# One planned, pinned order for every engine in a graph-attention plus gated-recurrence kernel

## The chip, the cores and the metric

The kernel runs on one core of a Trainium2 chip. A core has a matrix engine (TensorE, called PE in the profile, with its weight loads on a row called PEld), a vector engine (VectorE, DVE), a scalar engine (ScalarE, ACT), a general engine (GpSimd, POOL), and a sync engine (SyncE, SP) that here only issues transfers. The metric is the device time of one execution in microseconds (us). A span is one profiled execution, from its first to its last instruction.

## The reference, cut to what matters

There are 32 batch elements (B), each a table of 512 nodes by 128 features. One adjacency matrix of 512 by 512 zeros and ones serves all of them.

```python
# layer 0, for every batch element: graph attention
h = relu(layernorm(x))
hw = h @ W                                   # 512 x 128
logits = leaky_relu(hw @ a_src [rows] + hw @ a_dst [columns], 0.2)
alpha = softmax(logits where adj > 0)        # 512 x 512
x = x + leaky_relu(alpha @ hw + b, 0.3)
# layer 1, for every batch element: five gated recurrent steps
h = relu(layernorm(x))
for step in range(5):
    m = adj @ h
    z = sigmoid(m @ w3s.T + h @ u3.T)        # w3s: the two halves of w3 added, the same for w4, w5
    r = sigmoid(m @ w4s.T + h @ u3.T)
    hv = tanh(m @ w5s.T + (r * h) @ u5.T)
    h = (1 - z) * h + z * hv
out = x + h
```

The batch elements don't depend on each other, while the five steps of one element do. There are 160 such steps in all.

## The kernel before

**One step.** The state of an element is kept twice: transposed (`hT`, features on the partitions) and with nodes on the partitions, there split into a rounded part and the rest (`hi` and `lo`). `aggregate` multiplies `lo` and `hi` by the adjacency, eight matmuls into one PSUM bank (L573), and ACT copies the bank out as `mT` (L581). `gate_r` runs two products (L588, L589), a tanh (L591) and one vector operation that makes `rh` (L593). `candidate` adds the third product to the same bank (L599), takes its tanh (L603), and runs the two products of the candidate (L605, L606). `update` has one tanh (L614) and three vector operations that end in the new `hT` (L617 to L619). Then the state must be turned back to nodes on partitions. `turn` does it with four PE transposes (L635). `send` and `receive` do it with a vector transpose of 32 by 32 blocks (L643), one store to DRAM (L648) and four loads with rearranged addresses (L651), all on the SP queue. `halves` then makes `hi` on ACT (L419) and `lo` on DVE (L422), which the next `aggregate` reads.

**Layer 0** of an element is the generator `layer0`: a layer norm (L389 to L407, with one `pow` on POOL at L395), a transposition, a product (L474), scores `pt` (four vector operations, L511), the weighted average `av` (32 PE instructions, L528), its normalisation, a second layer norm, a second transposition and `halves`. The first four elements use PE transposes (`direct`); the others go through DRAM on the POOL queue (L431, L438), as does the row of exponentials `es` (L499, L504).

**What sets the order.** The driver at the end (L691 to L743) walks a software pipeline: in each turn one item is aggregated, the item before it goes through `gate_r`, the one before that through `candidate`, `update` and `send`, and after each third of a turn `advance` moves a layer 0 on by one piece. `WIDTH` = 6 elements run in the recurrence at once, `AHEAD` = 3 are in layer 0, and from `SENT` = 5 running elements on, the state is turned through DRAM. At the start three layer-0 generators are stepped in turn, `SKEW` = 3 pieces apart. This program order goes to the framework's scheduler, which makes each engine's instruction list from it with its own priorities and its own estimates of durations; only a few instructions are pinned to program order (`keep_in_program_order`: preparation of the adjacency, the input tests). Once made, the list of each engine is fixed, and an instruction that waits holds up those behind it in the list.

Of the kernel before, what the change touches and what calls it, by code (L numbers as in the profile page):

```python
# [21 lines left out]
SCORES = 25.0  # L22
WIDTH = 6
SENT = 5
SLOTS = 10
AHEAD = 3
DIRECT = 4
FIRST = 3
SKEW = 3
# [149 lines left out]
def gat_then_gated_gnn_kernel(  # L179
# [32 lines left out]
    xin = fast.enter_context(tc.tile_pool(name="xin", bufs=4))  # L212
    w2 = fast.enter_context(tc.tile_pool(name="w2", bufs=2))
    w3 = fast.enter_context(tc.tile_pool(name="w3", bufs=3))
    w4 = fast.enter_context(tc.tile_pool(name="w4", bufs=4))
    dram = fast.enter_context(tc.tile_pool(name="dram", bufs=4, space=bass.MemoryType.DRAM))
    psum = fast.enter_context(tc.tile_pool(name="psum", bufs=8, space=bass.MemoryType.PSUM))

    def bank(name):
        return psum.tile([P, N], F32, tag="bank", name=name)  # L220
# [11 lines left out]

    loaded = {}

    def load_x(b):
        if b < B:
            t = xin.tile([P, K, D], F32, tag="x", name=f"x_{b}")
            nc.sync.dma_start(out=t, in_=x_r[b])
            loaded[b] = t
# [21 lines left out]

    hws = [state.tile([P, K, D + 3], F32, name=f"hw_{s}") for s in range(AHEAD)]

# [9 lines left out]
    nc.scalar.dma_start(out=gw, in_=g_w)  # L273
    load_x(0)
    for i, v in enumerate((g_asrc, g_adst)):
        nc.scalar.dma_start(out=cols[:, i : i + 1], in_=v.rearrange("(d o) -> d o", o=1))
    nc.sync.dma_start(out=a_sb, in_=adj.rearrange("(p k) m -> p k m", k=K))
    load_x(1)
    nc.sync.dma_start(out=bias0, in_=g_b.partition_broadcast(P))
    load_x(2)  # L280
    for name, v in (("w3", w3_w), ("w4", w4_w), ("w5", w5_w)):
        nc.sync.dma_start(out=wide[name], in_=v)
    nc.sync.dma_start(out=u3, in_=u3_w)
    nc.sync.dma_start(out=u5, in_=u5_w)
    for i, v in enumerate((w3_b, w4_b, u3_b, w5_b, u5_b), 2):
        nc.sync.dma_start(out=cols[:, i : i + 1], in_=v.rearrange("(d o) -> d o", o=1))
    load_x(3)

    def prepare_layer0():

        wt_ps = bank("wt_ps")
        nc.tensor.transpose(wt_ps[:, :D], gw, ident)
        gwT = prep.tile([P, D], F32, name="gwT")
        nc.scalar.copy(gwT, wt_ps[:, :D])
        nc.gpsimd.tensor_copy(wrow[:, :D], gw)
        nc.gpsimd.tensor_copy(wsrc[:, :D], gw)
        wa_ps = bank("wa_ps")
        nc.tensor.matmul(wa_ps[:, 0:2], lhsT=gwT, rhs=cols[:, 0:2], start=True, stop=True)
        nc.scalar.copy(wa, wa_ps[:, 0:2])
        nc.scalar.copy(wrow[:, D : D + 1], wa[:, 1:2])  # L300
        nc.scalar.mul(wrow[:, D + 1 : D + 2], wa[:, 0:1], 0.8)
        nc.scalar.mul(wrow[:, D + 2 : D + 3], wa[:, 1:2], -0.8)
        nc.scalar.copy(wsrc[:, D : D + 1], wa[:, 0:1])
        nc.vector.tensor_scalar(wdst, ones, wa[:, 1:2], None, ALU.mult)

    def prepare_adjacency(c):

        at_ps = bank(f"at_ps{c}")
        for k in range(K):
            tc.keep_in_program_order(  # L310
                nc.tensor.transpose(
                    at_ps[:, ts(k, P)],
                    a_sb[:, k, :].rearrange("p (q c) -> p c q", c=K)[:, c, :],
                    ident,
                )
            )
        tc.keep_in_program_order(nc.vector.tensor_copy(adjT[:, c, :], at_ps))

    def prepare_layer1():


        sums = {}
        for name in ("w4", "w3", "w5"):
            sums[name] = prep.tile([P, D], F32, name=name + "s")
            nc.gpsimd.tensor_tensor(sums[name], wide[name][:, :D], wide[name][:, D:], ALU.add)
        nc.gpsimd.tensor_tensor(sums["w3"], sums["w3"], sums["w4"], ALU.subtract)
        t_ps = bank("w_ps")
        for i, name in enumerate(("w3", "w4", "w5")):
            nc.tensor.transpose(t_ps[:, ts(i, P)], sums[name], ident)
        nc.tensor.transpose(t_ps[:, ts(3, P)], u3, ident)  # L330
        for i, dst in enumerate((w3dT, w4sT, w5sT, u3T)):
            nc.scalar.copy(dst, t_ps[:, ts(i, P)])
        t_ps = bank("u5_ps")
        nc.tensor.transpose(t_ps[:, :D], u5, ident)

        tc.keep_in_program_order(
            nc.vector.tensor_scalar(u5hT, t_ps[:, :D], 0.5, None, ALU.mult)
        )
        tc.keep_in_program_order(
            nc.vector.tensor_scalar(zb, cols[:, 2:3], cols[:, 4:5], 0.5, ALU.add, ALU.mult)  # L340
        )
        tc.keep_in_program_order(
            nc.vector.tensor_scalar(rb, cols[:, 3:4], cols[:, 4:5], 0.5, ALU.add, ALU.mult)
        )
        tc.keep_in_program_order(
            nc.vector.tensor_tensor(vb, cols[:, 5:6], cols[:, 6:7], ALU.add)
        )

    def test_inputs():


        counts = prep.tile([P, 2 * K], F32, name="counts")
        for k in range(K):
            odd = w2.tile([P, N], F32, tag="d", name=f"odd_{k}")
            tc.keep_in_program_order(
                nc.vector.scalar_tensor_tensor(
                    odd, a_sb[:, k, :], 0.0, a_sb[:, k, :], ALU.not_equal, ALU.not_equal,
                    accum_out=counts[:, k : k + 1],
                )
            )  # L360
        deg = prep.tile([P, K], F32, name="deg")
        for k in range(K):
            tc.keep_in_program_order(
                nc.vector.tensor_reduce(
                    deg[:, k : k + 1], a_sb[:, k, :], mybir.AxisListType.X, ALU.max
                )
            )
        nc.vector.tensor_scalar(counts[:, K:], deg, 0.0, None, ALU.is_le)
        viol = prep.tile([P, 2], F32, name="viol")
        nc.vector.tensor_reduce(viol[:, 0:1], counts, mybir.AxisListType.X, ALU.add)  # L370
        wa2 = prep.tile([P, 2], F32, name="wa2")
        tc.keep_in_program_order(nc.vector.tensor_tensor(wa2, wa, wa, ALU.mult))
        nc.vector.tensor_reduce(viol[:, 1:2], wa2, mybir.AxisListType.X, ALU.add)
        return viol

    def conclude(viol):
        viol_ps = bank("viol_ps")
        nc.tensor.matmul(viol_ps[:, 0:2], lhsT=ones, rhs=viol, start=True, stop=True)
        over = prep.tile([P, 1], F32, name="over")
        nc.vector.tensor_scalar(over, viol_ps[:, 1:2], SCORES, None, ALU.is_gt)  # L380
        nc.vector.tensor_tensor(over, over, viol_ps[:, 0:1], ALU.add)
        nc.vector.tensor_scalar(flag, over, 0.0, None, ALU.is_gt)


    def relu_layernorm(dst, src, which, alone):
        st = w3.tile([P, K, 6], F32, tag="st", name=f"st_{which}")
        mv = w3.tile([P, K, 2], F32, tag="mv", name=f"mv_{which}")
        for k in range(K):
            nc.vector.bn_stats(st[:, k, :], src[:, k, :])  # L389
        for k in range(K):  # L390
            nc.vector.bn_aggr(mv[:, k, :], st[:, k, :])
        ve = w3.tile([P, K], F32, tag="ve", name=f"ve_{which}")
        nc.vector.tensor_scalar(ve, mv[:, :, 1], EPS, None, ALU.add)  # L393
        rs = w3.tile([P, K], F32, tag="rs", name=f"rs_{which}")
        nc.gpsimd.tensor_tensor(rs, ve, mhalf, ALU.pow)  # L395
        if alone:

            mean = mv[:, :, 0:1].to_broadcast([P, K, D])
            nc.vector.tensor_tensor(dst, src, mean, ALU.subtract)
            scale = rs.rearrange("p (k o) -> p k o", o=1).to_broadcast([P, K, D])  # L400
            nc.vector.scalar_tensor_tensor(dst, dst, 0.0, scale, ALU.max, ALU.mult)
            return

        nb = w3.tile([P, K], F32, tag="nb", name=f"nb_{which}")
        nc.vector.scalar_tensor_tensor(nb, mv[:, :, 0], -1.0, rs, ALU.mult, ALU.mult)
        for k in range(K):
            nc.scalar.activation(  # L407
                dst[:, k, :], src[:, k, :], AF.Relu, bias=nb[:, k : k + 1], scale=rs[:, k : k + 1]
            )

    def transposed(dst, src, which):
        t = bank(f"t_{which}")
        for k in range(K):
            nc.tensor.transpose(t[:, ts(k, P)], src[:, k, :], ident)
        nc.scalar.copy(dst, t)

    def halves(b, src, order="p k d -> p k d", **sizes):
        hi = his[b % SLOTS].rearrange(order, **sizes)
        nc.scalar.copy(hi, src)  # L419
        hi = his[b % SLOTS].bitcast(F32).rearrange(order, **sizes)  # L420
# [368 lines left out]
```

## Time and profile before

The median time is 1239.35 us (three runs, 1235.62 to 1241.69). The profiled span is 1236.1 us.

| engine | busy us | share of span | instructions |
|---|---|---|---|
| PE | 1168.6 | 95% | 4286 |
| PEld | 712.5 | 58% | 4286 |
| DVE | 936.7 | 76% | 2121 |
| ACT | 636.2 | 51% | 1260 |
| POOL | 346.5 | 28% | 496 |

Busy time by stage (us; the windows are cut from the start of the span):

| window | PE | DVE | ACT | POOL | granted PE clock |
|---|---|---|---|---|---|
| 0 to 100 | 73.23 | 61.39 | 45.35 | 24.36 | 0.96 |
| 100 to 250 | 134.80 | 101.25 | 68.74 | 42.73 | 0.96 |
| 250 to 1050 | 785.52 | 650.39 | 433.19 | 274.99 | 0.99 |
| 1050 to 1237 | 175.07 | 123.62 | 88.92 | 4.46 | 0.98 |

Busy time on PE counts overlapped matmuls generously: each of the 1280 instructions of L573 is shown as 399 or 474 ns long, while eight of them in a row take 1.84 us in the chain of waits.

### The profile page before, as it was taken

What the parts mean: (1) busy time and instruction counts of PE and PEld (TensorE: products, weight loads), DVE (VectorE), ACT (ScalarE), POOL (GpSimd) and SP (SyncE); (2) the same over time, 40 slices, a digit from 0 to 9 for tenths busy, and PEclk for the clock granted to TensorE, in tenths of its full rate; (3) what the DMA queues carried; (4) which work ended last, traced back from release to release, by engine and by line L of the source; (5) the groups of instructions that cost most, each with busy time, mean ns of one, the idle gap of its engine ahead of it and who ended that gap; (6) DMA issues with size and microseconds to landing.
All of it is one profiled execution on the core that took longest, in us unless ns stands there. A gap on an engine that the chain in (4) does not pass through costs nothing.

```text
span 1236.1 us, 15052 instructions
## 1 busy us (share of the span) xinstructions
PE 1168.6 (95%) x4286; PEld 712.5 (58%) x4286; DVE 936.7 (76%) x2121; ACT 636.2 (51%) x1260; POOL 346.5 (28%) x496
## 2 busy tenths in 40 slices
PE   6788887999999999999999999998999999999996
PEld 5555545655665655566566565655666666555553
DVE  5664667778788887888778887878888888766665
ACT  3454354455555555556544455555556545545552
POOL 2133132333334334233232333332332432100000
PEclk9899999999999999999999999999999999999998
DMA  3011123344444444353444443343443443322223
GB/s 95 20 44 34 26 61 111 111 129 119 135 129 129 128 120 131 103 146 106 126 122 128 140 127 116 113 136 112 128 130 118 128 120 113 109 94 85 86 88 119
DMA packets 134776, 133.40 MB, mean 108 GB/s; under 512 B 22432, under 2 KB 98592, under 8 KB 134560
## 3 DMA queue, kind: packets, MB, share of 16 engines
q1 hardware_dynamic: 116784, 95.54, 24.3%
q0 software_dynamic: 17472, 36.79, 12.0%
q8 instruction: 35, 0.57, 0.2%
q14 instruction: 53, 0.43, 0.1%
q10 hardware_dynamic: 432, 0.07, 0.0%
HBM read 70.65 MB, written 61.66 MB: 107 GB/s over the span
## 4 chain that ended last, share of the span: by engine, by line
PE 62%; DVE 17%; DMA 9%; POOL 4%; ACT 4%; issue 3%; SPq 1%; DVEq 0%; POOLq 0%; ACTq 0%
PE m L573 17%; PE g L588 8%; PE g L589 7%; PE v L606 7%; PE v L605 7%; PE g L599 7%; PE av L528 7%; DMA way<-blocks 3%; DMA rows<-way 3%; DVE lo L422 2%; DVE d L617 2%; DVE d L618 2%; DVE pt L511 2%; POOL rs_b L395 2%; DVE hT L619 1%
## 5 line engine op out<-in xcount | busy, mean ns | idle before, releaser
L573 PE MATMUL m<-adjT,lo 128*128 128x512 f32 x640 | 303.1, 474 | 25.8 <-DVE lo L422 25.8
L573 PE MATMUL m<-adjT,hi 128*128 128x512 f32 x640 | 255.3, 399 | 0.0
L591 ACT ACTIVATE rs<-g,rb 128x512 f32<-128x512 f32 x160 | 110.3, 689 | 150.9 <-PE g L589 148.5
L573 PEld LDWEIGHTS m<-adjT,lo 128*128 128x128 f32 x640 | 122.5, 191 | 89.0 <-DVE lo L422 32.0
L581 ACT COPY mT<-m 128x512 f32<-128x512 f32 x160 | 93.4, 584 | 148.5 <-PE m L573 148.1
L599 PE MATMUL g<-mT,w3dT 128*128 128x512 f32 x320 | 164.0, 594 | 1.7 <-ACT rs L591 1.6
L606 PE MATMUL v<-rh,u5hT 128*128 128x512 f32 x320 | 165.0, 597 | 0.0
L605 PE MATMUL v<-mT,w5sT 128*128 128x512 f32 x320 | 164.2, 595 | 0.0
L588 PE MATMUL g<-hT,u3T 128*128 128x512 f32 x320 | 164.1, 594 | 0.0
L589 PE MATMUL g<-mT,w4sT 128*128 128x512 f32 x320 | 163.4, 592 | 0.0
L593 DVE SCALAR_TENSOR_TENSOR rh<-rs,hT 128x512 f32<-128x512 f32 x160 | 108.0, 675 | 68.2 <-ACT rs L591 68.0
L614 ACT ACTIVATE hv<-v,vb 128x512 f32<-128x512 f32 x160 | 109.9, 687 | 93.4 <-PE v L606 92.3
L617 DVE TENSOR_TENSOR d<-hv,hT 128x512 f32<-128x512 f32 x160 | 109.3, 683 | 57.8 <-ACT hv L614 57.6
L528 PEld LDWEIGHTS av<-hw,pt 128*128 128x128 f32 x1024 | 129.0, 196 | 40.9 <-DVE pt L511 19.9
L573 PEld LDWEIGHTS m<-adjT,hi 128*128 128x128 f32 x640 | 122.8, 192 | 46.6 <-issue 23.1
L528 PE MATMUL av<-hw,pt 128*128 128x129 f32 x1024 | 132.7, 281 | 13.1 <-DVE pt L511 13.0
L395 POOL TENSOR_TENSOR rs_b<-ve_b,mhalf 128x4 f32<-128x4 f32 x32 | 36.4, 1137 | 344.5 <-DVE ve_b L393 222.6
L603 ACT ACTIVATE zs<-g,zb 128x512 f32<-128x512 f32 x160 | 110.1, 688 | 27.7 <-PE g L599 27.1
L419 ACT CAST hi<-rows 128x512 fp32r<-128x512 f32 x117 | 72.5, 619 | 87.1 <-DMA rows<-way 86.8
L619 DVE SCALAR_TENSOR_TENSOR hT<-d,hT 128x512 f32<-128x512 f32 x160 | 109.8, 686 | 9.0 <-DVE d L618 0.9
L618 DVE SCALAR_TENSOR_TENSOR d<-zs,d 128x512 f32<-128x512 f32 x160 | 109.7, 686 | 2.8
L643 DVE STREAM_TRANSPOSE blocks<-hT 128x512 f32<-128x512 f32 x147 | 103.9, 706 | 9.3 <-DMA way<-blocks 6.2
(115 smaller groups left out, 1391.2 us busy)
## 6 DMA issues: line engine op xcount, KB each, us to landing
way<-blocks SPq DMA_DIRECT2D x147, 256.0 KB, 2.1
rows<-way SPq DMA_DIRECT2D x588, 64.0 KB, 2.0
x<-in_x_dram SPq DMA_DIRECT2D x32, 256.0 KB, 2.7
out_dram<-res SPq DMA_DIRECT2D x32, 256.0 KB, 2.1
turn_a<-blocks_a POOLq DMA_DIRECT2D x112, 64.0 KB, 2.5
h0T<-turn_a POOLq DMA_DIRECT2D x28, 256.0 KB, 3.8
es<-line POOLq DMA_DIRECT2D x28, 256.0 KB, 3.9
turn_b<-blocks_b POOLq DMA_DIRECT2D x112, 64.0 KB, 2.4
```

The source lines that it names most:

```text
L528: nc.tensor.matmul(avs[:, i, :], lhsT=probs[c][:, ts(k, P)], rhs=hw[:, c, : D + 1], start=(c == 0), stop=(c == K - 1),)
L573: nc.tensor.matmul(m_ps, lhsT=part[b % SLOTS][:, k, :], rhs=adjT[:, k, :], start=(k == 0 and part is los), stop=(k == K - 1 and part is his),)
L588: nc.tensor.matmul(g_ps, lhsT=u3T, rhs=hT, start=True, stop=False)
L589: nc.tensor.matmul(g_ps, lhsT=w4sT, rhs=mT, start=False, stop=True)
L591: nc.scalar.activation(r, g_ps, AF.Tanh, bias=rb, scale=0.5)
L599: nc.tensor.matmul(g_ps, lhsT=w3dT, rhs=mT, start=False, stop=True, skip_group_check=True)
L603: nc.scalar.activation(z, g_ps, AF.Tanh, bias=zb, scale=0.5)
L605: nc.tensor.matmul(v_ps, lhsT=w5sT, rhs=mT, start=True, stop=False)
L606: nc.tensor.matmul(v_ps, lhsT=u5hT, rhs=rh, start=False, stop=True)
L617: nc.vector.tensor_tensor(d, hv, hT, ALU.subtract)
L618: nc.vector.scalar_tensor_tensor(d, z, 1.0, d, ALU.add, ALU.mult)
L619: nc.vector.scalar_tensor_tensor(hT, d, 0.5, hT, ALU.mult, ALU.add)
```

## The change

The driver, the generator and the lists of running elements go. Every piece of work becomes a `Task` with an engine, a length worked out from columns (`COST`: fixed nanoseconds, nanoseconds per column, time until the result is seen), a key (its urgency), the tasks it needs, and the buffers it takes or gives back. `plan` then plays the whole kernel through: it keeps a clock for each engine and a stock for each kind of buffer, always takes the engine that can begin first, and there, of the tasks that could begin at that moment, the one with the smallest key. The instructions are issued in that order, and all of them are pinned to it (`pin`), so that the framework's scheduler no longer chooses.

The computation stays the same. Besides the ordering, these details move: `aggregate` is two tasks, first the four matmuls of `hi`, then the four of `lo`; which steps are turned by PE transposes is a formula (the first few steps, and the last step of the last three elements) in place of a count of running elements; PSUM banks are planned by kind (`m` 2, `g` 3, `v` 2, the rest 4, of 8); the tests of the inputs move to the end of the run; the small input columns are loaded ahead of the first weights. The planner is told that each of the four loads of a sent state waits for the landing of the one before (`needs[-1:]`), and the same for stores on POOL; the instructions themselves have no such dependence.

```diff
+PACE = 3
 WIDTH = 6
-SENT = 5
 SLOTS = 10
-AHEAD = 3
+SHORT = 5
+SHORT_END = 3
+LEVEL = 8
+STEP = 6100
+LEAD = 11
+COST = {
+    "PE": (12, 0.413, 200),
+    "DVE": (70, 1.055, 140),
+    "ACT": (150, 0.83, 160),
+    "POOL": (650, 0, 130),
+    "SP": (430, 0, 0),
+}
+LANDING = 2600
+BANKS = {"m": 2, "g": 3, "v": 2, "o": 4, "bank": 8}
...
+def plan(tasks):
...
+            first = min(begins)
+            if best is None or first < best[0]:
+                t = min((t for t, b in zip(some, begins) if b == first), key=lambda t: t.key)
+                best = (first, t)
+        begin, t = best
...
+        free[t.engine] = begin + t.ns
+        seen = begin + t.ns + t.lands
...
+        order.append((begin, t))
+    return [t for _, t in order]
...
+    def due(b):
+
+        early = B - LEVEL
+        return 5 * b if b < early else 5 * early + PACE * (b - early)
+
+    def layer0(b):
+        direct = b < DIRECT
+        begin = (due(b) - LEAD * (0.6 if direct else 1)) * STEP
...
+    def recurrence(b, step, halved, turned):
+
+        key = (due(b) + WIDTH * step) * STEP
+        if b >= B - LEVEL:
+            key = min(key, (5 * B - LEVEL * (STEPS - 1 - step)) * STEP)
...
+        t = add("PE", [512] * K, keys(0), aggregate("hi", True), (high, *adjacency), (f_m,))
+        t = add("PE", [512] * K, keys(0), aggregate("lo", False), (t, low), (f_m,))
...
+        last = step == STEPS - 1
+        nth = 5 * b + WIDTH * step
+        if nth < 5 * SHORT or (last and b >= B - SHORT_END):
...
+            t = add("SP", [1], keys(6), store, (t,), (f_b, way), lands=LANDING)
+            needs = []
+            for g in range(G):
+                needs.append(add("SP", [1], keys(6), load(g), (t, *needs[-1:]), (way, f),
+                                 lands=LANDING))
...
-    while ready or waiting or coming or passing or any(pipeline):
...
-        if item:
-            aggregate(*item)
-        advance()
...
+    for t in plan(tasks):
+        t.issue()
```

## The prediction

> **What bounds the kernel now.** I read the page's busy shares first, then how far the recurrence got in each stretch of time, then the waits behind the slow stretches.
>
> ```profile
> PE 1168.6 (95%) x4286; PEld 712.5 (58%) x4286; DVE 936.7 (76%) x2121; ACT 636.2 (51%) x1260; POOL 346.5 (28%) x496
> PE 62%; DVE 17%; DMA 9%; POOL 4%; ACT 4%; issue 3%; SPq 1%; DVEq 0%; POOLq 0%; ACTq 0%
> ```
>
> PE looks full at 95%, but the chain of waits that ended last runs through PE for only 62%. So busy shares hide something, and I price PE by starts. In the chain eight matmuls of L573 take 1.84 us and each pair of L588, L589, L599, L605, L606 takes 0.86: a step costs 1.84 + 5 x 0.86 = 6.14 us. A layer 0 costs two `av` pieces of 1.79 plus eight `hp` instructions at about 0.11, so 4.5. A turn by four transposes takes 0.44. The whole demand on PE is 160 x 6.14 + 32 x 4.5 + 13 x 0.44 + some 8 for the transposes of preparation and of the first four elements: 982 + 144 + 6 + 8 = 1140 us. The span is 1236, so about 96 us pass in which PE isn't fed at full clock. That is all an ordering can win, and start and end keep part of it.
>
> Where they lie is seen in L573 alone, by stretches of 50 us (length, busy us and count, granted clock, DMA share, GB/s). Eight instructions are one step:
>
> ```profile
> 0.00:50.00 50.00, 4.43 (x12) 0.94 0.23 66
> 50.00:100.00 50.00, 11.75 (x41) 0.98 0.14 34
> 100.00:150.00 50.00, 12.74 (x46) 0.98 0.14 36
> 200.00:250.00 50.00, 14.89 (x48) 0.93 0.37 107
> ...
> 300.00:350.00 50.00, 16.22 (x56) 1.00 0.39 115
> ...
> 650.00:700.00 50.00, 13.99 (x49) 1.00 0.50 145
> ...
> 800.00:850.00 50.00, 13.50 (x48) 0.97 0.43 128
> ...
> 1100.00:1150.00 50.00, 19.89 (x68) 1.00 0.26 84
> ```
>
> A full stretch with layer 0 beside it holds 56, without layer 0 some 66. Pricing all PE lines in every stretch this way gives the loss by stage: 0 to 100 about 38 us, 100 to 250 about 22, 250 to 1050 about 19 (in a few dips), the end about 11. These sum to 90, the rest of the 96 being rounding and windows that cut a group.
>
> Next, what PE waited for over the whole run:
>
> ```profile
> PE m L573 <- DVE lo L422: 25.8, 15, 6.4
> PE av L528 <- DVE pt L511: 13.0, 14, 3.7
> ```
>
> The first is nearly all before 250 us (10.0 from 40 to 100, 14.4 from 100 to 250), the second is the dips. The timeline shows that both come from the order of lists, not from engines being full. At the start, DVE:
>
> ```profile
> 5.00 1.42 POOL L395 TENSOR_TENSOR rs_a<-ve_a,mhalf 128x4 f32<-128x4 f32 x1 [0.71 <-DVE ve_a L393]
> ...
> 8.06 0.87 DVE L389 BATCH_NORM_STATS2 st_a<-x 128x6 f32<-128x128 f32 x4 [2.55 <-DMA x<-in_x_dram]
> 8.85 0.36 DVE L391 BATCH_NORM_AGGREGATE mv_a<-st_a 128x2 f32<-128x6 f32 x4
> 9.13 0.66 DVE L401 SCALAR_TENSOR_TENSOR h<-h,rs_a 128x512 f32<-128x512 f32 x1
> ```
>
> The scale factor of element 0 is there at 6.42, but its use stands behind the statistics of element 1, whose input lands at 8.06: element 0 loses 2.7 us. In a dip, PE:
>
> ```profile
> 694.70 1.02 PE L606 MATMUL v<-rh,u5hT 128*128 128x512 f32 x2
> 697.94 0.49 PE L528 MATMUL av<-hw,pt 128*128 128x129 f32 x2 [2.21 <-DVE pt L511]
> 698.60 0.49 PE L528 MATMUL av<-hw,pt 128*128 128x129 f32 x2 [0.17 <-DVE pt L511]
> 698.85 0.48 PE L573 MATMUL m<-adjT,lo 128*128 128x512 f32 x1
> ```
>
> `av` waits for scores that wait for a transfer, while the step queued behind it has its `lo` ready since 687.88 (the DVE row at 687.20, 0.68 long).
>
> **What the Trainium skill says.** "Perfetto Trace Analysis", section "Identifying the Most-Contended Engine", says that matmul busy time misstates how near a kernel is to its limit, because pipelined matmuls overlap. The trace agrees: L599 is listed at 594 ns an instruction, and two of them take 0.86. "TensorE: Matmul & The Clock Gate", section "Architectural detail", says that matmuls keep program order, only weight loads move ahead, and that ACT and DVE queues are strictly first in, first out. The two timelines above show the cost: 2.2 us on PE, 2.7 us on DVE. The same page, section "What's actually happening", says that PE's clock falls to half after an idle window of about 3.4 us. The granted clock of 0.93 to 0.94 in two stretches above agrees in kind, so a wait costs more than its length.
>
> **The change part by part.**
>
> *Matmuls and vector work.* No product is added or removed. Turns by PE: the steps with 5b + 6 x step under 25 are 5 + 4 + 3 + 2 + 1 = 15, and three last steps, so 18 in place of 13. That adds 5 x 0.44 = 2.2 us to PE, and takes 5 blockwise transposes of 0.71 from DVE and 25 issues from SP, which is hidden: SP has slack and DVE is 81% busy in the middle (650 of 800).
>
> *Start, 0 to 250.* Before, element 0's first L573 begins at 36.3. I rebuild that chain from the same rows with no foreign work in it. x at 3.5, statistics 1.4, `pow` 1.4, scale 0.7 to 7; transposes and copy 1.2 to 8.2; product and scaling 2.5 to 10.7; spread 0.7; the adjacency lands near 8.5 and its 16 transposes and four casts take until about 14; the last scores 15; `av` 4 and its normalisation to 20; two vector operations 1.4, layer norm 3.6, `hi` 0.6: 25 to 26. With some collisions I take 28, 8 us earlier. The keys put elements 0, 1, 2 in that sequence, so each one's serial chain runs with priority and the others fill in. A step that turns by PE lasts 1.84 + 0.58 + 1.72 + 0.69 + 0.68 + 0.86 + 0.69 + 2.1 + 0.44 + 0.61 + 0.68 = 10.9 us, some 12.5 with hand-overs, for 6.14 of PE. Two to three elements therefore fill PE, and the third should be there near 45. I estimate the loss as 18 until 28, 9 from 28 to 60, 8 after that: 35 in place of 60. Gain **25**. The `hi` matmuls come first now, so PE starts 0.7 us (one `lo`) sooner in each such wait; that is inside the 25.
>
> *Middle, 250 to 1050.* 19 us lost in dips like the one shown. The planner's numbers are close to this trace: PE 12 + 0.413 x 2048 = 858 ns against 0.86, DVE 610 + 140 = 750 against 686, ACT 575 + 160 = 735 against 689, transfers 2.6 against medians of 2.0 to 2.7, 4.1 against 3.5 to 3.9. In the plan `av` is placed where its scores are ready, with a step ahead of it. I leave 8 for late landings (a `way` store took up to 5.5). Gain **11**.
>
> *Waits that it adds.* The loads of a sent state are planned one landing apart: 3.0 + 4 x 3.0 = 15 us for the round trip, where the trace has about 6 (2.1, four issues of 0.43, 2.0). Another element's store may stand between two loads on SP, and then these loads, the `hi` and `lo` behind them and the next aggregate wait for its DVE blocks. A step then lasts 11 + 15 = 26 us. Six running elements give it 6 x 7.0 = 42 us (56 counts of L573 in 50 us are 7.1 us a step). So it hides, at a price between 0 and the 15 us once at the change from PE turns to sent turns; I take 0.
>
> *End.* Three last turns by PE in place of two. After the last product the trace has 12.4 us (1223.6 to 1236). Of these 2.26 is the last result's wait for a buffer in use by an output. Gain **2** at most, say 1. The moved input tests (some 6 us of DVE) lie in the last part, where DVE is 66% busy: nothing.
>
> Sum: 25 + 11 + 1 - 2 = 35, so 1239.35 - 35 = **1204 us**.
>
> **The rivals.**
>
> *Start only.* The middle's stalls move instead of going, because landings vary and a pinned list can't react, no less than the old one. For it: `way` landings of 2.0 to 5.5 us. Against it: 15 us of slack in a round trip. Start gain of 15 to 25, middle 0: 1239 - 18 = about 1221.
>
> *Pinned queues cost more.* DVE is at 81% and everything passes through it, so one order for 2100 DVE instructions that is a little wrong makes PE wait in every step. The stocks (2 banks for `m`, 3 `rows`, 2 `blocks`) may bind as well when real lengths differ from planned ones. At half a DVE operation (0.35 us) a step, 160 x 0.35 = 56 lost against the 25 of the start: about 1270. For it: the trace before hardly shows what a tight pinned order does. Against it: long DVE, ACT and transfer times are planned above the measured ones, so real work tends to be early.
>
> *Nearly ideal.* Start loss 28, middle 3, end 9: 1140 + 2 + 28 + 3 + 9 + some 5 of clock: about 1187.
>
> **How the numbers follow.** Chances: forecast (1192 to 1214) 0.42, nearly ideal (1178 to 1192) 0.15, start only (1214 to 1233) 0.20, within 0.5% 0.03, pinned queues cost more (1246 to 1300) 0.20. Faster 0.77, same 0.03, slower 0.20. I leave out the far ends of the slow case and of the ideal one: 1182 to 1246.
>
> **What would show each step.** In the stretches of L573: about 16 or more in 0 to 50, 52 or more in 50 to 100, near 54 from 100 to 250, no stretch under 54 up to 1000. First L573 near 28. PE's waits for `lo` under 10 us in all, for scores under 5. 72 transposes of `h` and 142 `blocks`. Wrong it would be if PE showed a regular wait for `mT`, `rh` or a bank in each step, if SP's wait for `blocks` grew and `lo` came late in the middle, or if the first L573 stayed at 36.

## The result, and the profile after

| | before | after |
|---|---|---|
| time, median (us) | 1240.52 (1235.62 to 1241.7) | 1178.17 (1177.98 to 1179.46) |
| ratio, 95% interval | 1 | 0.9507 (0.9479 to 0.9535) |
| profiled span (us) | 1236.1 | 1176.3 |
| PE, busy share | 95% | 98% |
| granted PE clock, mean | 0.985 | 0.997 |

The change is faster by 62 us where 35 were forecast, and it lies 4 us below the range that was given. From the page of the kernel after, the busy shares:

```profile
PE 1148.4 (98%) x4306; PEld 704.8 (60%) x4306; DVE 928.6 (79%) x2114; ACT 644.5 (55%) x1260; POOL 351.2 (30%) x496
```

PE runs 20 instructions more and is busy 20 us less. The work didn't shrink; recorded lengths are not what a matmul costs. One of `av`, for instance, is listed at 281 ns before and 275 after, while its starts lie 112 ns apart in both. Again the progress of the recurrence, now line 882 (length, busy us and count, granted clock, DMA share, GB/s), eight instructions to a step:

```profile
0.00:50.00 50.00, 3.22 (x8) 0.97 0.23 69
50.00:100.00 50.00, 17.26 (x60) 1.00 0.17 45
100.00:150.00 50.00, 15.25 (x52) 1.00 0.16 41
...
200.00:250.00 50.00, 17.40 (x60) 1.00 0.49 133
...
300.00:350.00 50.00, 15.66 (x52) 1.00 0.42 122
...
650.00:700.00 50.00, 18.84 (x64) 1.00 0.40 120
...
800.00:850.00 50.00, 16.66 (x60) 1.00 0.42 118
...
1100.00:1150.00 50.00, 18.45 (x64) 1.00 0.33 104
```

From 50 to 1100 us every stretch is full or nearly so. A count of 52 is no dip here: in the plan a stretch that holds more `av` holds fewer steps, and the count jumps by whole steps. So I priced all PE lines in each stretch, as in the prediction, by the usual distance between starts in these traces (0.23 us for an instruction of L573 or L882, 0.429 for one of the five products, 0.1115 for `av`, 0.112 for `hp`, 0.11 for a transpose of a state), and took the sum from the length. Each instruction counts once, in the stretch in which it begins; the counts in the lines above show an instruction that crosses an edge in both stretches. What is left is the table that the rest of this text uses. The other 74 PE instructions, 8 us of transposes and the like at the start and end, count as loss in it:

| PE time not used (us) | 0 to 250 | 250 to 1050 | 1050 to the end | all |
|---|---|---|---|---|
| before | 69.6 | 25.2 | 12.0 | 106.7 |
| after | 29.6 | 3.0 | 12.1 | 44.7 |
| won | 40.0 | 22.2 | -0.1 | 62.0 |

The prices hold well: from 100 to 1100 us after the change, all but one of the 20 stretches come out within 0.4 us of full. The 20 added transposes take back 2.2 of the 62.0, and that leaves the 59.8 by which the spans differ, as it must. PE's waits over the run after:

```profile
PE wt_ps L404 <- DMA gw<-in_L_gnn_W_dram: 7.0, 1, 7.0
PE t_a L619 <- DVE h L587: 3.6, 1, 3.6
...
PE g L921 <- ACT rs L907: 1.6, 2, 0.8
PE m L882 <- ACT hi L859: 1.3, 1, 1.3
```

There is no wait for `lo` at all, where before had 25.8, and none for scores. The row of the weighted averages `av` in the list of groups ends in an idle time of 0.0, where the wait for scores stood:

```profile
L805 PE MATMUL av<-hw,pt 128*128 128x129 f32 x1024 | 124.0, 275 | 0.0
```

### The profile page after: what moved, and what is told of

The parts are those of the page before. It is cut to its first block, busy times and chain, and to the rows that moved or that the text cites. A ratio compares the mean times of both kernels' runs of the same rounds, so it can differ in the third digit from the quotient of the medians.

```text
span 1176.3 us, 14923 instructions
## 1 busy us (share of the span) xinstructions
PE 1148.4 (98%) x4306; PEld 704.8 (60%) x4306; DVE 928.6 (79%) x2114; ACT 644.5 (55%) x1260; POOL 351.2 (30%) x496
## 5 line engine op out<-in xcount | busy, mean ns | idle before, releaser
L882 PE MATMUL m<-adjT,lo 128*128 128x512 f32 x640 | 195.9, 438 | 0.0
L882 PE MATMUL m<-adjT,hi 128*128 128x512 f32 x640 | 191.1, 431 | 1.3 <-ACT hi L859 1.3
L882 PEld LDWEIGHTS m<-adjT,lo 128*128 128x128 f32 x640 | 119.0, 189 | 51.9 <-issue 29.9
L882 PEld LDWEIGHTS m<-adjT,hi 128*128 128x128 f32 x640 | 119.7, 189 | 50.3 <-issue 23.4
L805 PEld LDWEIGHTS av<-hw,pt 128*128 128x128 f32 x1024 | 123.4, 192 | 15.1 <-issue 12.4
L805 PE MATMUL av<-hw,pt 128*128 128x129 f32 x1024 | 124.0, 275 | 0.0
L857 DVE TENSOR_TENSOR lo<-rows,hi 128x512 fp32r<-128x512 f32 x114 | 77.9, 684 | 38.0 <-ACT hi L859 36.9
L938 PEld LDWEIGHTS v<-rh,u5hT 128*128 128x128 f32 x320 | 60.7, 190 | 78.0 <-issue 63.4
L902 PEld LDWEIGHTS g<-mT,w4sT 128*128 128x128 f32 x320 | 60.7, 190 | 76.7 <-issue 66.8
```

What stands on the lines that cost most here:

```text
L805: pin(nc.tensor.matmul(avs()[:, i, :], lhsT=f_pts[c].tile[:, ts(2 * part + i, P)], rhs=hw()[:, c, : D + 1], start=(c == 0), stop=(c == K - 1),
L882: pin(nc.tensor.matmul(f_m.tile, lhsT=part[:, k, :], rhs=adjT[:, k, :], start=(first and k == 0), stop=(not first and k == K - 1),))
L902: pin(nc.tensor.matmul(g, lhsT=w4sT, rhs=f_mT.tile, start=False, stop=True))
L938: pin(nc.tensor.matmul(v, lhsT=u5hT, rhs=f_rh.tile, start=False, stop=True))
```

## The experiments

**Two theories.** *The plan's order*: time is won because each list is made from true lengths, landings and urgency, so that nothing ready stands behind something that waits. *The pinning*: what hurt before was the framework's scheduler and its estimates, and any fixed order of the program would do. Smaller rivals are the split of the aggregate into `hi` and `lo`, the arrival of elements at the start, and the rule for PE turns. One reservation holds for all of them: any edit of the planner's numbers makes a new plan, and two plans can differ by some 5 us for no reason that was traced (seen in the last variants below). Effects of that size can't be put down to one cause.

### The order without the pins, and pins without the order

```diff
-    pin = tc.keep_in_program_order
+    pin = lambda ins: ins
```

> The planned order as program order, with no instruction pinned to it: the framework's scheduler may move things by its own estimates. If the gain lies in the plan's order, which already reaches the scheduler as program order, this stays near the change: 1178 to 1192. If it lies in the pinning, in that the scheduler's own reordering was what cost the time before, most of the 62 us come back: 1210 to 1240.

Measured: 1195.99 us (1195.24 to 1196.64), ratio 0.9656 (0.9622 to 0.9689). It fell between the two: the planned program order alone gives 44 of the 62 us, and pinning 18. In the table the loss is 33.6 up to 250, 19.9 in the middle and 8.9 at the end, against 29.6, 3.0 and 12.1 for the change, so what the scheduler moves costs in the middle.

The other half is the kernel before with every instruction pinned to its program order:

```diff
-    nc = tc.nc
+    nc = Pinned(tc)      # passes each instruction that it makes to tc.keep_in_program_order
```

> The kernel before with all its instructions pinned to its own hand-made program order, nothing planned. If the scheduler's reordering was the loss, this gains half of the change's 62 us or more: 1178 to 1210. If the plan's order is what counts, a pinned order that knows no lengths is no better than before and rather worse: 1235 to 1300, with PE waiting for lo and for scores at least the 39 us of before.

Measured: 1731.41 us, ratio 1.3983 (1.3933 to 1.4033). PE's longest wait in this run:

```profile
PE m L184 <- DVE lo L184: 301.7, 71, 17.8
```

(Line 184 is the wrapper's, so the names tell.) The wait for `lo` grew from 25.8 to 301.7 us. So pinning as such is no gain, and this old program order does better when the scheduler moves its pieces. The pinning theory, that any fixed order of the program would do, falls.

### What the plan must know: urgency

```diff
-        key = (due(b) + WIDTH * step) * STEP
+        key = b              # and the same for every task of the element
```

> The change with every task's key set to the number of its element, so that the oldest element always goes first and the paced urgency (a place every 5 steps, layer 0 begun 11 steps ahead) is gone; lengths, landings and buffers are planned as before. If the lengths and landings carry the gain, the plan finds other work for PE whatever the keys are, up to the end, where the last elements run alone: 1180 to 1195. If the keys carry it, layer 0 of new elements is put off until PE starves: 1210 or more.

Measured: 1244.52 us (1241.16 to 1247.95), ratio 1.0022: the whole gain is gone, though lengths, landings and buffers are planned as in the change. The wait, and two stretches of the recurrence:

```profile
PE m L880 <- ACT hi L859: 31.2, 14, 9.9
```

```profile
150.00:200.00 50.00, 11.12 (x40) 0.93 0.36 98
...
1200.00:1244.00 44.00, 8.72 (x24) 0.77 0.09 31
```

The old elements are served first until few are left. In the timeline of ACT the `hi` of new elements is made at 32.1, 50.9, 59.8, 64.9 and then not before 174.95 us; with the change's keys the fifth comes at 111.25. The plan knows that PE will run dry, but it picks only by the key and doesn't look ahead. The last stretches are thin, as the last line shows: 38 us of loss after 1150, where the change has 9.

### What the plan must know: landings and lengths

A landing is the time from a transfer's issue until its data are there.

```diff
-LANDING = 2600
+LANDING = 0              # and no 1500 for the loads that spread
```

> The change with a planner that believes every transfer through DRAM lands at once (0 in place of 2.6 us, 0 in place of 4.1 us). If the known landing times are what took the waits out of the middle, they come back: PE waits for scores and for hi or lo of 15 to 40 us, 1193 to 1220. If six elements in flight give enough slack whatever the planner believes, 1176 to 1183.

Measured: 1566.01 us, ratio 1.2647 (1.2603 to 1.2692). The direction was expected, the size was not. ACT's longest wait in this run, and then the same wait in the change:

```profile
ACT hi L859 <- DMA rows<-way: 528.8, 114, 9.3
```

```profile
ACT hi L859 <- DMA rows<-way: 8.4, 9, 2.3
```

One such wait in the timeline of the landing-free plan (start, length, in brackets the idle time before and its end):

```profile
610.23 0.62 ACT L859 CAST hi<-rows 128x512 fp32r<-128x512 f32 x1 [6.83 <-DMA rows<-way]
610.76 0.58 ACT L893 COPY mT<-m 128x512 f32<-128x512 f32 x1
...
611.39 1.13 PE L902 MATMUL g<-mT,w4sT 128*128 128x512 f32 x2 [2.43 <-ACT mT L893]
```

ACT stands 6.83 us in front of a cast whose rows haven't landed. The copy of another element's `mT` is behind it, and PE waits 2.43 us for that copy. PE's longest wait over this run is again one for ACT:

```profile
PE g L921 <- ACT rs L907: 145.4, 42, 7.6
```

A cast that waits and holds up the copy behind it: that is the strict first-in, first-out queue of ACT that the Trainium skill states ("TensorE: Matmul & The Clock Gate", section "Architectural detail"), and this trace agrees, with 6.83 us at the cast and 2.43 behind it.

Then the landings too short by less, with the loads and stores planned side by side:

```diff
-LANDING = 2600
+LANDING = 1000           # and no 1500 for the loads that spread
-                needs.append(add("SP", [1], keys(6), load(g), (t, *needs[-1:]), (way, f),
+                needs.append(add("SP", [1], keys(6), load(g), (t,), (way, f),
```

> The change with unchained loads and stores, and landings of 1.0 us in place of 2.6 (and of 4.1): a round trip is planned at about 4 us where the trace has 6 to 7. If an error of two or three us in a round trip is covered by the six elements in flight: 1174 to 1185. If the plan must not be early by any transfer, since each queue then waits in order for a landing: 1210 or more, between the change and the 1566 of the planner that knows no landings.

Measured: 1366.58 us, ratio 1.0998 (1.0945 to 1.1052). Being early by two to three us in a round trip of about 6, and by about three in the loads on POOL, is enough to lose the gain three times over.

And side by side alone, with landings of 2.6 kept:

```diff
-                needs.append(add("SP", [1], keys(6), load(g), (t, *needs[-1:]), (way, f),
+                needs.append(add("SP", [1], keys(6), load(g), (t,), (way, f),
```

(The same for the two kinds of stores on POOL.)

> The change with a planner that lets the four loads (and the four stores on POOL) go side by side: a round trip is planned at about 7 us, close to the 6 us of the trace, in place of 15. If the surplus of 8 us is the slack that takes up late landings, PE's waits come back in part: 1186 to 1200. If the plain landing time is enough, no change, or a little better since a step is shorter: 1174 to 1181.

Measured: 1173.7 us (1173.14 to 1174.7), ratio 0.9457 (0.9419 to 0.9496). No surplus is needed: a plan of about 7 us for the trip has no regular waits either. It is 4.8 us under the second measurement of the change (1178.46, below), 2.9 of them after 1050 (9.2 lost there, against 12.1). Whether the chain of the change costs this in general is open: on top of another variant, below, the same edit lost 2.3 us.

The lengths of DVE and ACT, 30% shorter and 10% longer than in the change:

```diff
-    "DVE": (70, 1.055, 140),
-    "ACT": (150, 0.83, 160),
+    "DVE": (49, 0.739, 98),       # and in the longer variant: (77, 1.16, 154)
+    "ACT": (105, 0.581, 112),     # and in the longer variant: (165, 0.913, 176)
```

> The change with a planner that takes DVE and ACT operations for 30% shorter than they are (fixed part, per column and time to be seen), transfers as in the change. If exact lengths of all engines carry the gain, PE's waits for rh, rs and mT come back in each step: 1200 to 1260. If only transfers matter, because they are the long waits and six elements in flight cover 0.2 us per operation: 1176 to 1186.

> The change with a planner that takes DVE and ACT operations for 10% longer than in the change (30% shorter cost 105 us). If a plan only must not be early, because an in-order list that waits holds up ready work, while a late entry costs idle time only where nothing else was placed: 1178 to 1188. If any error in the lengths costs alike, a third of the error gives about a third of the loss: 1205 to 1220.

Measured: 1283.77 us for the short ones (ratio 1.0341, 1.0308 to 1.0374), 1181.37 for the long ones (0.9513, 0.9483 to 0.9543). The change plans a DVE operation at 750 ns until its result is seen, where the trace has about 686; so the short lengths, 525 ns, are 23% under the trace, and not 30% as the expectation says. They lose 84 us from 250 to 1050, and PE's longest wait is this one:

```profile
PE g L921 <- ACT rs L907: 38.8, 21, 3.6
```

This fits a plan in which PE comes to the third product when `rs` should be there and isn't, so that everything PE has behind it waits. Lengths 10% longer cost 3 us in all, 30% shorter ones 105. A run with 10% too short would be the exact counterpart, and was not made.

### The smaller rivals

The aggregate as one task, `lo` and `hi` alternating as before:

```diff
-        t = add("PE", [512] * K, keys(0), aggregate("hi", True), (high, *adjacency), (f_m,))
-        t = add("PE", [512] * K, keys(0), aggregate("lo", False), (t, low), (f_m,))
+        t = add("PE", [512] * (2 * K), keys(0), aggregate, (high, low, *adjacency), (f_m,))
```

> The change with each aggregate as one task again, lo and hi alternating, begun only when both are there. If the gain lies in the plan, which moves other work ahead of a step that isn't ready, this costs little: 1178 to 1184. If the wait for lo went away because hi goes first, PE waits for lo come back, some 15 us or more of the 25.8 us of before: 1193 to 1205.

Measured: 1185.68 us (1184.98 to 1186.0), ratio 0.957 (0.9537 to 0.9603). The split is worth 7 us, more than expected by the plan's theory and half of the rival's least. The wait for `lo` comes back only in part:

```profile
PE m L879 <- DVE lo L857: 5.1, 3, 3.9
```

No state turned by PE:

```diff
-        if nth < 5 * SHORT or (last and b >= B - SHORT_END):
+        if False:
```

> The change with no state turned by PE: all 160 go through DRAM, the first steps and the last ones too. If PE turns at the start are what keeps PE fed from 50 to 250 us, the first steps, now some 10 to 15 us longer, leave PE idle: 1190 to 1205. If elements that arrive early do it, PE saves 18 turns of 0.44 us and loses about as much at both ends: 1174 to 1186, the last one costing 5 us or so at the end.

Measured: 1187.11 us, ratio 0.9566 (0.9527 to 0.9604), just over the second expectation. The loss up to 250 us is 35.0 in place of 29.6, and after 1050 it is 25.0 in place of 12.1, while 18 turns of 0.44 are saved. PE turns matter at the end more than at the start.

The inputs of element 3 held back to 54 us and those of later elements to 88 us:

```diff
-        load = add("SP", [1], 5 * (b - LEAD) * STEP if not first else b - 9e9, issue, (), (f,),
-                   lands=max(3000, at))
+        load = add("SP", [1], 5 * (b - LEAD) * STEP if not first else b - 9e9, issue, (), (f,),
+                   lands=max(3000, at), at=0 if b < 3 else 54000 if b == 3 else 88000)
```

> The change with the inputs of element 3 held back to 54 us and those of element 4 and later ones to 88 us, so that their layer 0 ends about when it did before (92 and 135 us, in place of 65 and 111). If the 35 us won between 50 and 250 us come from elements arriving earlier, most of them are lost again: 1198 to 1213, with PE waiting for hi or lo. If they come from the order of the work that is there, the time stays under 1188.

Measured: 1188.34 us (1187.81 to 1191.66), ratio 0.9584 (0.9543 to 0.9625), just over the bound of the second expectation and 10 us short of the first. With `hi` of element 3 at 92.3 and of element 4 at 158.7 (before: 91.7 and 134.9) the loss up to 250 is 37.5 in place of 29.6. Late arrival explains 8 to 10 us of the 40, and with element 4 later than it was before, this is rather too much than too little. From the other side, the kernel before with four elements begun at the start:

```diff
-FIRST = 3
+FIRST = 4                # and a fourth buffer for their products
```

> The kernel before with four in place of three layer 0 begun at the start (and a fourth buffer for their products), so that element 3 reaches the recurrence earlier than at 92 us. If late arrival of elements made the loss of 35 us between 50 and 250 us, 8 us or more are won: under 1231. If the order of each list made it, the loss stays or grows: 1236 to 1260.

Measured: 1236.15 us, ratio 0.9953 (0.9938 to 0.9968), which is better by 5 to 6 us and less than the arrival theory asked for. But the whole time hides two opposite moves. Element 3 arrives at 82.0 in place of 91.7, and the loss up to 250 us falls by 11.5, from 69.6 to 58.1. PE still waits for `lo` between 50 and 250 us (24.4 before, from 40 on):

```profile
PE m L573 <- DVE lo L422: 13.0, 8, 3.5
```

From 250 to 1050 the loss rises by 9.9, from 25.2 to 35.1, where PE now waits 10.5 us for `lo` (1.4 before) and 10.1 for the transfer of `h0T` (none before).

So earlier arrival is worth some 11 us where it happens, and the lists that the scheduler then made lose most of it again.

### The start with measured landings

In the change's own trace the start has two faults of the kind that the prediction had found in the old one (POOL, DVE and PE):

```profile
6.90 0.29 POOL L410 COPY wrow<-gw 128x128 f32<-128x128 f32 x1 [5.58 <-DMA gw<-in_L_gnn_W_dram]
7.39 1.04 POOL L578 TENSOR_TENSOR rs_a<-ve_a,mhalf 128x4 f32<-128x4 f32 x1
9.92 0.87 DVE L566 BATCH_NORM_STATS2 st_a<-x 128x6 f32<-128x128 f32 x4 [3.61 <-DMA x<-in_x_dram]
11.18 0.69 DVE L587 SCALAR_TENSOR_TENSOR h<-h,rs_a 128x512 f32<-128x512 f32 x1
11.92 1.12 PE L619 MATMUL t_a<-ident,h 128*128 128x128 f32 x4 [3.55 <-DVE h L587]
```

The plan has the weights at 4.5 us, and they land at 6.9, so POOL's `pow` stands behind their copy. It has the input of element 3, issued after the whole adjacency, landing 3.0 us after its issue. It lands at 9.92, 7.3 us after, and element 0's scaling stands behind it.

```diff
-    firsts = (3000, 7000, 7500)
+    firsts = (3900, 4500, 4700)    # element 3: 7750 after its issue; first weights at 6900
```

> The changed kernel itself once more, beside its variants on the same chip, as the yardstick for them: 1177 to 1180.

> The change with the landing times of the first loads as its own trace shows them (inputs of elements 0 to 3 at 3.9, 4.5, 4.7 and 7.75 us after issue, first weights at 6.9 us). In the trace of the change the input of element 3 is planned too early, its statistics stand ahead of element 0's scaling, and POOL's pow stands behind copies of weights that land at 6.9: element 0's first transposes begin at 11.9. If such wrong entries cost what the chain says, these begin near 8 to 9 and the whole is 2 to 4 us shorter: 1174 to 1176. If PE's idle time at the start is bound by later parts of the chain, under 1 us changes.

Measured: the change again at 1178.46 us (1178.2 to 1179.46), this variant at 1178.73 (1176.71 to 1180.24), so no gain. The first transposes do begin at 8.21:

```profile
8.21 1.12 PE L619 MATMUL t_a<-ident,h 128*128 128x128 f32 x4
```

The loss up to 250 us falls from 29.6 to 24.3, but the end (from 1050) loses 17.1 in place of 12.1. In PE's waits from 1100 on, the one for `hT` before a turn is 5.9 us in place of 2.8. Why this plan ends so was not traced further.

Both improvements at once (the edits of the start and of the unchained loads):

> Measured landings at the start together with unchained loads and stores. If the two gains lie in different places (start; buffers and the end), they add up: 1170 to 1172. If they overlap: 1173 to 1175.

Measured: 1181.06 us (1179.42 to 1183.14), a miss for both expectations. The start keeps its gain (25.5 up to 250), but the middle now loses 14.5 in place of 3.0, in small waits, of which PE has 6.8 us for `rh` over the run. Why this plan has them and the one with unchained loads alone does not was not settled.

And the measured start with one setting moved:

```diff
-LEAD = 11
+LEAD = 13
```

> Measured landings at the start with layer 0 begun 13 steps ahead in place of 11. With 11, the start of this variant loses 6 us less than the change, and its end 11 us more (20.7 against 9.1 us of PE in the last stretch), so that nothing is won. If that end is an accident of how the last elements fall together, another lead removes it and the gain of the start is seen: 1168 to 1174. If the end gives back whatever the start wins: 1177 to 1181.

Measured: 1173.78 us (1173.12 to 1174.61), ratio 0.9449 (0.942 to 0.9478). The expectation's 20.7 us for the last stretch were taken over 32 us where only 26.2 are in the span; counted to the span's end it was 15.8, against 9.2 in the change. Here it is 8.6, and the gain of the start is seen. This and the unchained loads alone are the best of the runs, 4.7 and 4.8 us under the change, and none of their times overlaps with those of the change, though each was measured on another chip. The variants of this part also show how far a plan moves without a traced reason: a lead of 13 in place of 11 took 5 us off, and the unchained loads took off 4.8 us on the change but added 2.3 on the measured start.

## Why the prediction was wrong

**The bound was right.** PE's demand of 1140 us fits: the table's 106.7, less the 8 us of other PE instructions that the 1140 include, is 98.6, against the 96 that the prediction had left to win. 72 transposes of `h` and 142 `blocks` came as counted, and none of the regular waits named as signs of a failure appeared. Two of the signs were not met: 8 instructions of the aggregate in the first 50 us where about 16 were named, and stretches of 48 to 53 later, which are full all the same. The direction and the mechanism were right, and two terms of the sum, the gains of the start and of the middle, were sized too small.

**Start: 25 us forecast, 40.0 measured.** The step that failed is "I estimate the loss as 18 until 28, 9 from 28 to 60, 8 after that". Its base was right: with the 8 us set apart, as the prediction has them, 61.4 were lost before, and 60 was put. What stays after the change is 21.7 and not 35: 15.8 until 28 (the same as before the change), 5.6 from 28 to 60, and 0.3 from 60 to 250. The first L882 begins at 33.0 and not at 28, some 3 us of it because of the two faults shown above (30.1 with the measured landings), but other PE work lies ahead of it, so the first term held all the same. The last two failed. The prediction took a shortage for granted until elements are many, as the old trace had it. After the change two to four elements, with the `av` of others, fill PE from 50 us on. Arrival accounts for 8 to 11 us of the 40, by the run with late inputs and the one with four elements first. The rest is the order of the lists; how it divides between them was not separated.

**Middle: 11 us forecast, 22.2 measured.** Two terms failed. The base, "19 us lost in dips like the one shown", should have been 25.2: the counts by stretches hold an instruction that crosses an edge twice, some 0.5 us at each of 16 edges, and this hid 6 to 8 us of loss. And "I leave 8 for late landings (a `way` store took up to 5.5)": 3.0 are left. The plan with unchained loads has 1.7 left with a round trip planned at 7 us, so it was not the surplus that took the late landings up. What the runs show is that the planned length decides: with landings planned at 1.0 us, 142.9 us are lost in the middle. That one late landing delays only one element while the lists hold enough of the others is the likely reason, and was not tested by itself.

**End: 1 forecast, -0.1 measured.** As sized, within the error of the prices.

**The added wait: 0 taken.** The variant without it is 4.8 us faster, mostly at the end, where the prediction put a price between 0 and 15 "once at the change from PE turns to sent turns". That is within what two plans differ by, so a cost isn't shown.

**The rivals.** *Nearly ideal* (1187) came closest and was given 0.15. Its 3 for the middle is what was measured; its start of 28 should have been 21.7, its end of 9 came out at 12.1, and its 5 for the clock isn't needed. *Pinned queues cost more* did not come about, but its picture, an order that is a little wrong and makes PE wait, is what the runs with short landings and short lengths show: 1367 to 1566 and 1284. That the planned lengths lay above the measured ones was noted in the prediction as speaking against this rival, and with lengths longer by a further 10% the time is still 1181. The prediction gave that argument too little weight.

## What to carry to other kernels

Read the dips of the bounding engine by stage, and for each ask whether ready work stood behind something that waited: if it did, a better list can win nearly the whole dip and not half of it (22.2 of 25.2 us in the middle here). Count an instruction that crosses the edge of a stretch only once. An order fixed for in-order queues must rest on lengths and landings that are true or somewhat long, since being early by a few us in a transfer cost three to six times the gain here. It also needs urgency that brings new work in before the old runs out: the same plan by age alone won nothing. A difference of 5 us between two such plans says little about the edit that made it.

## What was not expected of the hardware

The granted clock of PE stays at 1.00 in every stretch from 50 to 1150 us after the change. Before, eight of these 22 stretches had 0.93 to 0.98. In six of the eight PE had a wait of 1.9 to 6.4 us, and the other two follow a stretch with one of 2.2 or 3.0; the five other stretches with waits, none over 2.2 us, kept 1.00. Over whole runs the mean clock falls with the loss: 0.997 with 44.7 us lost, 0.985 with 106.7, 0.958 with 237 and 0.914 with 432. So long waits and a lower clock come together in these traces; what the lower clock costs by itself was not separated. A 256 KB input issued right behind the 1 MB adjacency landed 7.3 us after its issue, while such loads took 2.8 us in the median.
